# Adding a residual with accumulating scatters, and a new order on GpSimd, in a two-layer graph kernel

## The chip, the cores and the metric

The kernel runs on one core of one Trainium2 chip. The metric is the device time of one execution in microseconds (us). The core has five instruction queues of its own: TensorE (PE in the profile), VectorE (DVE), ScalarE (ACT), GpSimd (POOL) and SyncE (SP). Each works through its queue in order. DMA transfers are issued from GpSimd (all indexed ones) and from SyncE (all plain ones).

## The reference, cut to what matters

There are 16 graphs (batches) of 1024 nodes with 64 channels. Layer 0 adds a weighted mean over neighbours. Layer 1 takes, for each node and channel, three quantiles over the values of its neighbours, after some edges are removed ("dilation"), and sends the result through a small MLP. Both layers add to x.

```python
h = relu(layernorm(x))
deg = clip(sum(A, axis=2, keepdims=True), 1.0)
x = x + matmul(A / deg, h)                       # layer 0: the residual x1
h = relu(layernorm(x))
adj_d = dilate(adj, mask)                        # drops edges; the own node stays
agg = sum(w * nanquantile(h over neighbours, tau)
          for tau, w in zip([0.25, 0.5, 0.75], [0.25, 0.5, 0.25]))
y = relu((h + agg) @ W1 + b1) @ W2 + b2
x = x + y * mask                                 # the output
```

## The kernel before

**Layer 0** (`loads`, `beginnings`, `transposes`, `products`, `signs`, `listing`, `endings`, `channels`, lines 540 to 777) goes batch by batch. Rows of the adjacency matrix are loaded in eight tiles `at`; TensorE transposes them into `pt`, ScalarE copies them to `att`, TensorE multiplies by the normed x (`ps_small<-att,h`). VectorE scales, adds x and so has the residual x1. ScalarE makes signs `sg` of the rows, from which VectorE takes the largest eight keys of each of four segments (MAX8, `rec`): a list of each node's neighbours. For each node one record `row` is built (line 568): normed channels and two place holders (W = 66 columns), then x1 (64 columns, `X1`), then the list with number and mask (34 columns, `R0`), 164 in all (`RW`). The first 66 columns go to the table `tab` in HBM with a plain store (lines 710 to 712). The whole record is scattered into `srt[g]`, rows ordered by length of list (`to`, lines 773 to 775): eight indirect DMAs for each batch, 128 in all, called row scatters below. Four batches make a group (GB = 4), so there are four groups g.

**Layer 1, short lists** (`group`, line 1015). When all batches of a group are scattered, the lists come back (`recs`), the node numbers `nodes_i` are computed, GpSimd gathers the adjacency rows of the longest short lists (`gat_rows`), VectorE computes the indices `idx` and which edges go, and two indirect stores into `tab` write the dropped edges (`tab<-drop,didx`). Then ten `Job`s for each group are added (line 1126), each of T tiles of 128 nodes with n - 1 neighbours. `Job.run` (line 808) loads the own rows `S` from `srt` on SyncE, gathers T(n - 1) tiles of `places` from `tab` on GpSimd, one indirect DMA each, and then `sort` (line 840) runs a sorting network on VectorE between `places` and `other` (in PSUM) and multiplies by weights into `prod`. `layers` (line 960) does the MLP: TensorE transposes and sums `prod` into `pt`, ScalarE copies to `ot`, TensorE multiplies, ScalarE applies the activation (`hid`), TensorE multiplies, and ScalarE scales by the mask into `y`. Then VectorE adds x1 from `S` to y (line 1006) and GpSimd scatters y into the output, T indirect DMAs of 128 rows of 256 bytes (line 1011): 128 of these in all. `S` is held until the add.

**Layer 1, long lists** (`long_lists`, line 1133). Nodes with up to 88, 31, 24 and 20 neighbours, of all four groups, make four further jobs. For each, SyncE loads the records `lS`, VectorE computes `lnodes_i`, GpSimd gathers the adjacency rows (`lat`, one buffer), VectorE takes the neighbours out of them (`lkey`, `lfound`, `lkeys`, `lidx`), and a job gathers `lplaces`.

**What sets the order.** The engine queues are in order, and on VectorE and GpSimd the order is written out by the kernel's own planner (`Plan`, lines 233 to 325), when the program is built. Each piece of work is a stream that yields an engine, a time at which it may begin, and a rank. `Plan.run` always takes the stream that can begin first by the planner's clocks, and among those that can begin at the same time the one of lowest rank. Constants are slack added to the time at which an input is due: SLACK (2 us), LOOSE (15) ahead of the MLP and of the add, ROWS (7) ahead of row scatters and index gathers, LATE (25) ahead of the scatters of y. AHEAD (8) decides when a sort is urgent: `later` gives it a low rank while fewer than so many gathers are outstanding. `room(name, bufs)` holds a stream until a buffer is free.

Of the kernel before, what the change touches and what calls it, by code (L numbers as in the profile page):

```python
# [9 lines left out]
F32 = mybir.dt.float32  # L10
# [8 lines left out]
P = 128  # L19
# [189 lines left out]

INF = float("inf")  # L210
BREATH = 0.8
AHEAD = 8
SLACK = 2.0
LOOSE = 15.0
ROWS = 7.0
LATE = 25.0


class Timed:
# [13 lines left out]
class Plan:  # L233
# [132 lines left out]
def list_path(ctx, tc, x, adj, nodemask, w1, b1, w2, b2, out, go):  # L366
# [9 lines left out]
    W = C + 2  # L376
    PW = W // 2
    REC = 8 * NSEG + 2
    X1 = W
    R0 = X1 + C  # L380
    RW = R0 + REC
    NTAU = N // SUB
    NF = NG + NG + len(LONG)

# [173 lines left out]
    def beginnings(pool, now):  # L558

        for b, st in enumerate(batch):  # L560
            now[0] = b
            yield "DVE", lambda: max(known(st, "xt", "mrow"), room("h0", 3), room("row", 4))
            mrow_f = new(tiny, [NT, P], F32, "mrow_f", 2)
            nc.vector.tensor_copy(mrow_f, st["mrow"])

            h0 = new(pool, [P, NT, C + 1], F32, "h0", 3, users=2)
            nc.vector.memset(h0[:, :, C:], 1.0)
            row = st["row"] = new(pool, [P, NT, RW], F32, "row", 4, users=1)
# [89 lines left out]
    def products(pool, now):  # L658


        for b, st in enumerate(batch):
            now[0] = b
            for hf in range(2):
# [25 lines left out]
                x1 = st["row"][:, hf * BPH:(hf + 1) * BPH, X1:R0]  # L689
# [13 lines left out]
    def channels(pool, now):  # L703

        for b, st in enumerate(batch):
            now[0] = b
            row = lambda: st["row"]
            yield "DVE", lambda: known(st, "row") if st["residual"] == 2 else INF
            yield from normed(row()[:, :, :C], row()[:, :, X1:R0])
            nc.sync.dma_start(  # L710
                tab[b * TS:b * TS + N, :].rearrange("(t p) w -> p t w", p=P), row()[:, :, :W]
            )
            st["normed"] = True

    def endings(pool, now):

        for b, st in enumerate(batch):
            now[0] = b
            g, gb = divmod(b, GB)
# [51 lines left out]
            to = new(pool, [P, NT], I32, "to", 2)  # L771
            nc.vector.scalar_tensor_tensor(to, low, float(1 - GB), pos, op0=OP.mult, op1=OP.add)
            for t in range(NT):
                yield "POOL", lambda: max(at(to), at(row)) + ROWS if "normed" in st else INF
                scatter(srt[g], row[:, t, :], to[:, t:t + 1], sorts[g])
            free(row)
            progress["batches"] = b + 1

# [4 lines left out]
            in_offset=bass.IndirectOffsetOnAxis(ap=idx, axis=0),  # L783
        )

    def scatter(dst, src, idx, others):
        if plan.last is others:
            nc.gpsimd.memset(turn, 0.0)
        ins = nc.gpsimd.indirect_dma_start(
            out=dst, out_offset=bass.IndirectOffsetOnAxis(ap=idx, axis=0),  # L790
            in_=src, in_offset=None,
        )

        for other in others:
            tc.declare_no_dep(ins.ins, other, reason="rows of their own")
        others.append(ins.ins)
        plan.last = others

    class Job:
# [1 line left out]


        def __init__(self, pool, n, T, keys, idx, node, mask, nodes_i, table, S, g, name="places",
                     bufs=3, rank=0):
            self.__dict__.update(locals())
            self.short = pool is gat

        def run(self):
# [9 lines left out]
            progress["ahead"] += T * (n - 1)  # L818
            if short:
                mine = self.S  # L820
                self.S = new(pool, [P, T, R0], F32, "S", 4, users=1)
                nc.sync.dma_start(self.S, mine)
            for t in range(T):
                for k in range(n - 1):
# [11 lines left out]
        def later(self, rank):  # L836

            return rank - 900 if progress["ahead"] < AHEAD else rank + 2000

        def sort(self):  # L840
            n, T, pool, short, A, S = self.n, self.T, self.pool, self.short, self.A, self.S
# [101 lines left out]
            if short:  # L943
                free(A)
                free(Bt)
                yield "ACT", lambda: at(S)
                nc.scalar.copy(prod[:, :, count, :], S[:, :, :C])

                terms = [
                    [prod[:, t, k:min(k + 2, total), :].rearrange("p k c -> p (k c)")  # L950
                     for k in (0, *range(4, total, 2), 2)]
                    for t in range(T)
                ]
                plan.add(self.layers(terms, [prod]), -1000)
            else:
                terms = [[places(copies[k], (k, 1, 1, 1, 1))[:, 0, 0, :] for k in range(count)]
                         + [S[:, 0, :C]]]
                plan.add(self.layers(terms, [A, Bt]), -1000)

        def layers(self, terms, sources):  # L960

            T, R = self.T, terms[0][0].shape[1]
            yield "PE", lambda: max(at(*sources) + LOOSE, room("y", 6), room("pt", 2))
            y = new(mlp, [P, T, CO], F32, "y", 6, users=1)
            for t0 in range(0, T, 4):
                ts = range(t0, min(t0 + 4, T))
                M = len(ts) * P
# [34 lines left out]
                        y[:, t, :], pv[:, i, :], AF.Copy, scale=self.mask[:, t:t + 1]  # L1002
                    )
                free(py)
            yield "DVE", lambda: at(y) + LOOSE
            nc.vector.tensor_tensor(y, y, self.S[:, :, X1:R0], OP.add)
            if self.short:
                free(self.S)
            for t in range(T):
                yield "POOL", lambda: at(y) + LATE  # L1010
                scatter(out_rows, y[:, t, :], self.nodes_i[:, t:t + 1], scatters)
            free(y)
            progress["jobs"][self.g] += 1

    def group(g):
# [17 lines left out]
        )  # L1033
        nodes_i = new(grp, [P, NTAU], I32, "nodes_i", 2)
        nc.vector.tensor_copy(nodes_i, nodes)
        yield "POOL", lambda: at(nodes_i) + ROWS
        full = new(grp, [P, N], F32, "gat_rows", 1)
        gather(full, adj_rows, nodes_i[:, 0:1])
        yield "DVE", always
# [65 lines left out]
        for e in range(2):  # L1105
# [1 line left out]
                nb, cum, skip[:, e, :], None, op0=OP.is_lt, op1=OP.add,  # L1107
                accum_out=drop[:, 0, e:e + 1],
            )
        yield "POOL", lambda: at(drop) + ROWS  # L1110
        for e in range(2):
            nc.gpsimd.indirect_dma_start(
                out=pairs[:R * TS * PW, :],
# [9 lines left out]
        for i, ts in enumerate(classes):  # L1123
            n, T = CAPS[ts[0]] + 1, len(ts)
            sl = slice(ts[0], ts[-1] + 1)
            job = Job(
                gat, n, T, keys[:, sl, :n - 1], idx[:, sl, :], node[:, sl], mask[:, sl],
                nodes_i[:, sl], table, tiles[:, sl, :R0], g,
            )
            plan.add(job.run(), 100 * g + i)  # L1130
        progress["groups"] = g + 1

    def long_lists(pool):
# [4 lines left out]
        for l, K in enumerate(LONG):  # L1138
# [12 lines left out]
            nc.vector.tensor_tensor(nodes, node, noff[:, 1:2], OP.add)  # L1151
            nodes_i = new(pool, [P, 1], I32, "lnodes_i", 4)
            nc.vector.tensor_copy(nodes_i, nodes)
            yield "POOL", lambda: max(at(nodes_i) + ROWS, room("lat", 1))
            full = new(pool, [P, N], F32, "lat", 1)
            gather(full, adj_rows, nodes_i)
            yield "DVE", lambda: at(full)
# [367 lines left out]
```

## Time and profile before

Three runs took 1947.86, 1949.79 and 1966.94 us; the median is 1949.79 us. The profiled execution spans 1953.2 us.

| | TensorE | VectorE | ScalarE | GpSimd |
|---|---|---|---|---|
| busy, us | 818.3 | 1252.1 | 607.3 | 965.2 |
| share of the span | 42% | 64% | 31% | 49% |

The costliest groups on GpSimd are indirect DMAs, each as one instruction: gathers of `places` (496 of 994 ns), of `lplaces` (163 of 1057 ns), row scatters (128 of 980 ns), scatters of y (124 of 1045 ns, and four for the long lists). Busy time by slices of the span, in tenths, each slice being 48.8 us:

```profile
PE   6778651345688236611577001000001458142155
DVE  7766877636676557954642396747935779785290
ACT  7888744225465435513333000000000011010011
POOL 0123255534434654347525625478775546747723
```

A digit is the busy share of the engine in that slice. The first 22 slices hold layer 0, with the short lists of the earlier groups beside it. After that ScalarE and TensorE have little to do. In a group's row, the time after "idle before" is what the engine stood idle just ahead of those instructions, and the names after the arrow say what ended it; "issue" is a wait for nothing that the profile shows.

### The profile page before, as it was taken

What the parts mean: (1) busy time and instruction counts of PE and PEld (TensorE: products, weight loads), DVE (VectorE), ACT (ScalarE), POOL (GpSimd) and SP (SyncE); (2) the same over time, 40 slices, a digit from 0 to 9 for tenths busy, and PEclk for the clock granted to TensorE, in tenths of its full rate; (3) what the DMA queues carried; (4) which work ended last, traced back from release to release, by engine and by line L of the source; (5) the groups of instructions that cost most, each with busy time, mean ns of one, the idle gap of its engine ahead of it and who ended that gap; (6) DMA issues with size and microseconds to landing.
All of it is one profiled execution on the core that took longest, in us unless ns stands there. A gap on an engine that the chain in (4) does not pass through costs nothing.

```text
span 1953.2 us, 15147 instructions
## 1 busy us (share of the span) xinstructions
PE 818.3 (42%) x3336; PEld 518.3 (27%) x3336; DVE 1252.1 (64%) x4090; ACT 607.3 (31%) x1874; POOL 965.2 (49%) x1140
## 2 busy tenths in 40 slices
PE   6778651345688236611577001000001458142155
PEld 3334421223355013410245000000001237132134
DVE  7766877636676557954642396747935779785290
ACT  7888744225465435513333000000000011010011
POOL 0123255534434654347525625478775546747723
PEclk8978875667788678755777555555555557555556
DMA  4545633213344323422201201111111101111100
GB/s 159 160 123 167 182 103 83 64 47 75 93 123 126 91 77 117 105 74 60 56 23 37 56 19 32 30 40 22 24 27 36 25 17 25 25 43 32 24 7 14
DMA packets 119013, 129.09 MB, mean 66 GB/s; under 512 B 68306, under 2 KB 86866, under 8 KB 118914
## 3 DMA queue, kind: packets, MB, share of 16 engines
q1 hardware_dynamic: 86178, 86.58, 15.6%
q0 software_dynamic: 32736, 41.47, 9.4%
q14 instruction: 71, 0.58, 0.1%
q8 instruction: 28, 0.46, 0.1%
HBM read 108.70 MB, written 19.28 MB: 66 GB/s over the span
## 4 chain that ended last, share of the span: by engine, by line
DVE 34%; PE 16%; issue 15%; another core or an unknown queue 14%; ACT 9%; POOL 8%; DMA 2%; SPq 0%; DVEq 0%; POOLq 0%; ACTq 0%
PE ps_small L227 9%; PE pt L227 7%; DVE other L227 5%; DVE places L227 5%; DVE rec L227 4%; POOL lplaces L227 3%; POOL places L227 2%; DVE lplaces L227 2%; DVE long_other L227 2%; ACT ln_sq L227 2%; ACT sg L227 2%; DVE sg L227 2%; POOL out_dram L227 2%; ACT att L227 2%
## 5 line engine op out<-in xcount | busy, mean ns | idle before, releaser
L227 POOL DMA_INDIRECT places<-tab,idx x496 | 493.1, 994 | 263.6 <-issue 141.7
L227 PE MATMUL pt<-ident,prod 128*128 128x128 f32 (+1 forms) x736 | 155.7, 371 | 553.1 <-DVE prod L227 350.2
L227 PE MATMUL ps_small<-att,h 128*65 128x512 f32 x512 | 269.8, 677 | 63.3 <-ACT h L227 42.8
L227 PEld LDWEIGHTS pt<-ident,prod 128*128 128x128 f32 (+1 forms) x736 | 127.2, 254 | 586.0 <-issue 210.5
L227 PE MATMUL pt<-ident,at 128*128 128x128 f32 x1024 | 184.9, 329 | 170.8 <-ACT att L227 83.5
L227 POOL DMA_INDIRECT srt<-row,to x128 | 125.4, 980 | 261.0 <-ACT row L227 158.6
L227 POOL DMA_INDIRECT out_dram<-y,nodes_i x124 | 129.6, 1045 | 210.9 <-issue 72.2
L227 POOL DMA_INDIRECT lplaces<-tab,lidx x163 | 172.3, 1057 | 73.0 <-issue 47.8
L227 PEld LDWEIGHTS pt<-ident,at 128*128 128x128 f32 x1024 | 139.6, 167 | 225.0 <-ACT att L227 106.8
L227 DVE MAX8 rec<-sg 128x8 f16<-128x256 f16 x512 | 180.2, 414 | 13.2 <-remote 5.8
L227 ACT COPY att<-pt 128x512 f32<-128x512 f32 x256 | 142.3, 583 | 130.9 <-remote 79.8
L227 ACT COPY ot<-pt 128x128 f32<-128x128 f32 (+3 forms) x56 | 22.4, 399 | 426.6 <-issue 175.3
L227 ACT ACTIVATE sg<-at 128x1024 f16<-128x1024 f32 x128 | 134.9, 1055 | 40.8 <-DVE rec L227 19.0
L227 DVE TENSOR_TENSOR sg<-sg,keyed 128x1024 f16<-128x1024 f16 x128 | 87.3, 682 | 81.0 <-ACT sg L227 80.8
L227 PEld LDWEIGHTS ps_small<-att,h 128*65 128x65 f32 x512 | 78.7, 159 | 208.8 <-issue 137.8
L227 PE MATMUL ps_small<-ot,w_sb 128*128 128x128 f32 (+3 forms) x112 | 56.9, 602 | 121.7 <-ACT ot L227 89.1
L227 DVE TENSOR_TENSOR other<-places,other 128x64 f32<-128x64 f32 (+6 forms) x204 | 69.8, 342 | 39.3 <-DVE places L227 11.6
L227 PE MATMUL ps_small<-w_sb,hid 128*128 128x64 f32 x256 | 68.6, 360 | 58.4 <-issue 43.0
L227 ACT ACTIVATE y<-ps_small,recs 128x64 f32<-128x64 f32 x124 | 31.5, 312 | 187.2 <-PE ps_small L227 66.3
L227 ACT ACTIVATE wu<-wu 128x39 f32<-128x39 f32 (+9 forms) x40 | 9.4, 235 | 249.7 <-issue 130.5
L227 DVE TENSOR_TENSOR places<-places,other 128x64 f32<-128x64 f32 (+2 forms) x208 | 62.4, 309 | 25.4 <-DVE other L227 10.2
L227 PEld LDWEIGHTS ps_small<-w_sb,hid 128*128 128x128 f32 x256 | 51.1, 246 | 87.7 <-issue 53.3
(208 smaller groups left out, 1652.2 us busy)
## 6 DMA issues: line engine op xcount, KB each, us to landing
at<-in_adj_dram SPq DMA_DIRECT2D x128, 512.0 KB
places<-tab,idx POOLq DMA_INDIRECT x496
tab<-row SPq DMA_DIRECT2D x16, 264.0 KB
xt<-in_x_dram SPq DMA_DIRECT2D x16, 256.0 KB
S<-srt SPq DMA_DIRECT2D x8, 390.0 KB
lplaces<-tab,lidx POOLq DMA_INDIRECT x163
recs<-srt SPq DMA_DIRECT2D x4, 544.0 KB
S<-srt SPq DMA_DIRECT2D x8, 260.0 KB
```

Source lines behind the costliest of these rows:

```text
L227: ins = getattr(self._engine, op)(*args, **kwargs)
```

## The change

The residual x1 no longer travels with the ordered rows. When a batch's x1 is finished it is written to the output with a plain store on SyncE, 256 KB for each batch; the scatter of y becomes one that adds to what stands there (`compute_op=OP.add`), and VectorE's add goes. It is meant to take that add and its waits off VectorE. Since the scatter now depends on what was written before, it names only the part of the output up to its own group, so that it doesn't depend on batches still to come. The record is 100 columns wide for the ordered rows instead of 164, `S` 66 instead of 130, and `S` is free as soon as it has been copied into `prod`.

Beside this, `places` has four buffers instead of three and `y` four instead of six. The slack constants become one, LOOSE = 7 (from 15, 7 and 25), and the index gathers have none. AHEAD is 16. Row scatters get a rank ahead of everything that can begin at the same time (`first`), and the MLP of a short job is urgent only while fewer than 16 gathers are outstanding (`urgent`), and otherwise last; before, it always had rank -1000.

```diff
-AHEAD = 8
+AHEAD = 16
 SLACK = 2.0
-LOOSE = 15.0
-ROWS = 7.0
-LATE = 25.0
+LOOSE = 7.0
...
-    X1 = W
-    R0 = X1 + C
-    RW = R0 + REC
+    R0 = W
+    X1 = RW = R0 + REC
...
-            yield from normed(row()[:, :, :C], row()[:, :, X1:R0])
+            yield from normed(row()[:, :, :C], row()[:, :, X1:])
+
+            nc.sync.dma_start(out[b].rearrange("(t p) c -> p t c", p=P), row()[:, :, X1:])
...
+        first = lambda rank: rank - 3000
...
-                yield "POOL", lambda: max(at(to), at(row)) + ROWS if "normed" in st else INF
-                scatter(srt[g], row[:, t, :], to[:, t:t + 1], sorts[g])
+                yield "POOL", lambda: max(at(to), at(row)) + LOOSE if "normed" in st else INF, first
+                scatter(srt[g], row[:, t, :RW], to[:, t:t + 1], sorts[g])
...
-    def scatter(dst, src, idx, others):
+    def scatter(dst, src, idx, others, op=OP.bypass):
...
-            in_=src, in_offset=None,
+            in_=src, in_offset=None, compute_op=op,
...
-                     bufs=3, rank=0):
+                     bufs=4, rank=0):
...
-                self.S = new(pool, [P, T, R0], F32, "S", 4, users=1)
+                self.S = new(pool, [P, T, W], F32, "S", 4, users=1)
...
+        def urgent(self):
+            return -1000 if progress["ahead"] < AHEAD else 5000
...
                 nc.scalar.copy(prod[:, :, count, :], S[:, :, :C])
+                free(S)
...
-                plan.add(self.layers(terms, [prod]), -1000)
+                plan.add(self.layers(terms, [prod]), self.urgent)
...
-            yield "PE", lambda: max(at(*sources) + LOOSE, room("y", 6), room("pt", 2))
-            y = new(mlp, [P, T, CO], F32, "y", 6, users=1)
+            yield "PE", lambda: max(at(*sources) + LOOSE, room("y", 4), room("pt", 2))
+            y = new(mlp, [P, T, CO], F32, "y", 4, users=1)
...
-            yield "DVE", lambda: at(y) + LOOSE
-            nc.vector.tensor_tensor(y, y, self.S[:, :, X1:R0], OP.add)
-            if self.short:
-                free(self.S)
             for t in range(T):
-                yield "POOL", lambda: at(y) + LATE
-                scatter(out_rows, y[:, t, :], self.nodes_i[:, t:t + 1], scatters)
+                yield "POOL", lambda: at(y) + LOOSE
+                rows = out_rows[:min(self.g + 1, NG) * GB * N, :]
+                scatter(rows, y[:, t, :], self.nodes_i[:, t:t + 1], scatters, OP.add)
...
-        yield "POOL", lambda: at(nodes_i) + ROWS
+        yield "POOL", lambda: at(nodes_i)
...
-        yield "POOL", lambda: at(drop) + ROWS
+        yield "POOL", lambda: at(drop)
...
-            yield "POOL", lambda: max(at(nodes_i) + ROWS, room("lat", 1))
+            yield "POOL", lambda: max(at(nodes_i), room("lat", 1))
```

More of the change, by code (lines that the diff above doesn't have):

```diff
@@ L567, in beginnings @@
             nc.vector.memset(h0[:, :, C:], 1.0)
-            row = st["row"] = new(pool, [P, NT, RW], F32, "row", 4, users=1)
+            row = st["row"] = new(pool, [P, NT, X1 + C], F32, "row", 4, users=1)
             nc.vector.memset(row[:, :, C:W], -1.0)
@@ L688, in products @@
                 yield "DVE", lambda: at(pb) + SLACK
-                x1 = st["row"][:, hf * BPH:(hf + 1) * BPH, X1:R0]
+                x1 = st["row"][:, hf * BPH:(hf + 1) * BPH, X1:]
                 deg = new(tiny, [P, BPH], F32, "deg", 2)
@@ L1127, in group @@
                 gat, n, T, keys[:, sl, :n - 1], idx[:, sl, :], node[:, sl], mask[:, sl],
-                nodes_i[:, sl], table, tiles[:, sl, :R0], g,
+                nodes_i[:, sl], table, tiles[:, sl, :W], g,
             )
```

## The prediction

> **What bounds the kernel now.** I read the page's busy times and chain first, then busy time by stage, then the waits, then GpSimd's timeline where the stages meet. In the page (parts 1 and 4) the reader is to see that no engine is full and the chain is spread over all of them.
>
> ```profile
> PE 818.3 (42%) x3336; PEld 518.3 (27%) x3336; DVE 1252.1 (64%) x4090; ACT 607.3 (31%) x1874; POOL 965.2 (49%) x1140
> ...
> DVE 34%; PE 16%; issue 15%; another core or an unknown queue 14%; ACT 9%; POOL 8%; DMA 2%; SPq 0%; DVEq 0%; POOLq 0%; ACTq 0%
> ```
>
> The stages differ, so I cut the span at four events: the last row scatter (1077 us), the first sort of the 88-place list (1328), the last gather (1871), the end.
>
> ```profile
> core 0: us, PE busy (x) PEld busy (x) DVE busy (x) ACT busy (x) POOL busy (x), PEclk, DMA share, GB/s
> 0.00:1077.00 1077.00, 593.61 (x2380) 342.37 (x2380) 679.62 (x2271) 546.83 (x1681) 451.03 (x589) 0.73 0.35 97
> 1077.00:1328.00 251.00, 14.21 (x50) 11.55 (x50) 154.78 (x572) 4.93 (x18) 134.55 (x152) 0.50 0.15 35
> 1328.00:1871.00 543.00, 164.22 (x688) 128.21 (x688) 384.55 (x1149) 40.77 (x130) 354.35 (x357) 0.56 0.14 27
> 1871.00:1954.00 83.00, 46.23 (x219) 36.14 (x218) 33.15 (x99) 14.81 (x45) 25.30 (x44) 0.64 0.04 11
> ```
>
> A (layer 0 beside the short lists of three groups): four engines at 42 to 63%, held by waits for each other. B and C: VectorE and GpSimd alone, taking turns. D: a drain. The waits say how they take turns:
>
> ```profile
> POOL places L227 <- DVE prod L227: 112.2, 10, 16.7
> ...
> POOL out_dram L227 <- DVE y L227: 62.2, 5, 26.1
> ...
> DVE y L227 <- ACT y L227: 58.4, 10, 18.3
> ```
>
> GpSimd waits for a free buffer of places (112 us) and for finished y (62 us), and VectorE, in order, for y from ScalarE (58 us). Then the boundaries, in the timelines of GpSimd and VectorE:
>
> ```profile
> 1137.99 0.94 POOL L227 DMA_INDIRECT gat_rows<-in_adj_dram,nodes_i  x1 [25.31 <-DVE nodes_i L227]
> ...
> 1167.99 0.99 POOL L227 DMA_INDIRECT tab<-drop,didx  x1 [15.05 <-DVE lkeys L227]
> ...
> 1228.28 0.94 POOL L227 DMA_INDIRECT lat<-in_adj_dram,lnodes_i  x1 [16.74 <-DVE lnodes_i L227]
> ...
> 1271.96 0.94 POOL L227 DMA_INDIRECT lat<-in_adj_dram,lnodes_i  x1 [17.43 <-DVE other L227]
> ...
> 1328.41 0.34 DVE L227 TENSOR_TENSOR lrem<-lplaces,lS 128x176 f32<-128x176 f32 x1 [20.19 <-DMA lplaces<-tab,lidx]
> ...
> 1871.10 1.02 POOL L227 DMA_INDIRECT places<-tab,idx  x1 [0.30 <-issue]
> ...
> 1916.63 0.96 POOL L227 DMA_INDIRECT out_dram<-y,nodes_i  x1 [26.07 <-DVE y L227]
> ```
>
> In B GpSimd stands four times (74 us together) for indices from VectorE, and then VectorE for the last gathers of the long list. In D it stands for y.
>
> **What the Trainium skill says.** "DMA: Bandwidth & Descriptors", SWDGE vs HWDGE vs iDMA: accumulation in a DMA can only be issued by GpSimd, and a DMA operation is one read and one write descriptor. It gives no price for the added read of the destination; no run so far shows one. The same page, Rules for kernel authors: an accumulating DMA must wait for any earlier access of the same bytes; so each scatter depends on the plain write of its batches. The same page, Anatomy of one DMA: about 2.0 us fixed, mostly the receipt of the write; the trace agrees (2.18 us from the last row scatter to its landing). The same page, Specifications: under 512 B a transfer is not at line rate; row scatters go from 656 to 400 B, but the DMA share is 0.04 to 0.35, so I cost it at nothing.
>
> **The change, part by part.**
>
> The add leaves VectorE. 44 instructions of y<-y,S and y<-y,lS at a median 0.354 us and less: about 14 us of busy time. More is in the waiting: the 58.4 us above is VectorE at the head of its queue, with lists and sorts behind it. Of it 18.3 us (at 1785 to 1803) lay where VectorE starved for gathers anyway, 21 us (7.3 and 13.7) is at the very end.
>
> Residual writes: 16 plain writes of 256 KB on SyncE's queue; the rows shorten the sorted stores, and the loads of S, by about as much. DMA share at most 0.35: nothing.
>
> Stage B. I compared the built order of GpSimd's 931 indirect DMAs. The last row scatter is number 443 before, 441 after; the last gather for the 88-place list 578 and 576: the same work lies between. But the gather of the last group's adjacency rows moves from 471 to 456, its two stores from 483-484 to 474-475, the second to fourth gathers of lat from 492, 514, 535 to 483, 500, 516. On VectorE (each instruction at its row's mean) the lists now stand 25, 26 and 25 us apart, before 33, 31, 21, and the last group's nodes come 27 us of work after layer 0 instead of 41, with the first job of that group behind them. Walked from the last row scatter (t): lists load and first lnodes t+13 as now; nodes t+28 (now t+61); the two stores 26 us of work later, t+54; second lat 15 us on, t+70; the next two 25 us of list work and about 2 us of latency each, t+124; then 60 DMAs. GpSimd ran them in C at (545-94)/331 = 1.36 us each, where 94 us is its idle time over 1 us: 82 us, t+206, landed t+208. Now it is t+251. Gain 43 us; between 20 (if half is met by new stalls) and 50.
>
> Stage C. From the last gather of that list to the last gather of all: 338 DMAs instead of 331, +9.5 us. The fourth buffer of places lets GpSimd run one job further: of the 94 us idle, 56 us are waits on prod (11.8+15.2+5.3+9.3+4.5+10.0). I take off 30: VectorE must then do some 415 us in 520, 80%; from 1500 to 1800 us it reached 75 to 80%. Net -20; ends -45 and +10.
>
> Stage D. After the last gather 17 scatters remain instead of 22, and only the two smallest jobs, some 10 us of VectorE, instead of the 37 us to its last prod at 1908. The rest I take as now: 25 us from prod to y, 3 us, 9 us to the end. 2+10+25+3+9 = 49 us for 83, -34; ends -45 and -10.
>
> Stage A. Row scatters first, later layers behind gathers (urgent), slack of 7 for 15 and 25. Group 1's lists stand at 364 us of VectorE work instead of 427, so jobs spread more evenly over layer 0. Against it, TensorE meets the first prod after 7.0 batches of transposes instead of 8.0, while VectorE gets to it after the same 240 us of work; TensorE already waits 28 us there. The ends of the stage agree (700 and 709 us of VectorE work, the 8 us being adds). -10; ends -70 and +70.
>
> The accumulating scatter: 128 of them, now 0.96 us each. Lower bound: nothing, the fixed cost of issue rules. Upper: twice as much to write out, +0.96 us. I take +0.25, on the path in B to D where GpSimd is half the bound: about 63 x 0.25 = +16; ends 0 and +60.
>
> Sum: -43-20-34-10+16 = -91, so 1950-91 = 1859 us.
>
> **The rivals.** (1) The gain is hidden: VectorE's chains of small dependent steps set stage C, and GpSimd running ahead changes nothing; B gives 20, D 10, adds 5 or so: about 1925 us. For it: at 1474 to 1490 VectorE steps at 1.4 us for operations of 0.23. Against: 74 us of stalls in B have named causes that move. (2) The accumulating scatter costs double: +60 instead of +16, and A loses 35 by blocked gathers behind it: 1938 us. For it: every scatter holds GpSimd's queue. Against: gather and scatter cost the same 0.94 to 0.96 us now, whatever they move. (3) Slower: with slack of 7 GpSimd arrives at scatters whose y is late, as already at 1008 us (30.7 us of idle time), and TensorE stands at prod earlier: A +70, B to D give 35: 1985 us. For it: in A it is GpSimd's in-order waits for y that hold later gathers. Against: y no longer goes through VectorE, whose add came up to 28 us after y's first write (311.6 to 339.3).
>
> **How the numbers follow.** Forecast 0.54, hidden 0.17, double cost 0.11, slower 0.18. Faster by over 1% (below 1930): forecast and hidden, 0.71; within 1%: 0.11; slower: 0.18. The low end adds the good ends of B, C, and part of A: about 1780. The high end takes in rivals 1 and 2 and reaches into 3: 1970.
>
> **What would show it.** The last row scatter near 1067 (A), the first lrem some 208 us later (B), the last gather some 520 us after that with less wait on prod (C), the end within 50 us (D). Scatters into the output of about 1.2 us on GpSimd. No wait of VectorE on y. It is wrong if the last row scatter comes after 1110, if scatters take near 2 us, or if waits of GpSimd for y grow past what prod waits lose.

## The result and the profile after

The changed kernel took 1829.05 us (median of 4 runs, 1823.34 to 1833.25). The kernel before, run again beside it, took 1956.74 us (4 runs, 1947.86 to 1966.94). The ratio is 0.9345, with an interval from 0.9303 to 0.9387: 6.5% faster. The forecast was 1859 us with a range from 1780 to 1970, so the direction and the range held and the time came 30 us lower. The sum came out closer than its terms did.

The page of the changed kernel, engine by engine, and its group for the scatters of y:

```profile
PE 825.6 (45%) x3336; PEld 533.0 (29%) x3336; DVE 1240.1 (68%) x4046; ACT 609.3 (33%) x1874; POOL 1050.8 (58%) x1144
...
L225 POOL DMA_INDIRECT out_dram<-y,nodes_i x124 | 208.0, 1678 | 186.8 <-ACT y L225 127.4
```

VectorE has 44 instructions fewer, the adds, which took 15.2 us before; its busy time fell by 12 us. GpSimd's rose by 85.6 us: the 124 scatters now take 1678 ns each on the mean where they took 1045. The same four stages as before, cut at the last row scatter (988 us), the first `lrem` of the 88-place list (1215), the last gather (1779) and the end; the columns are the stretch, its length, and busy time and instructions of the five engines, then granted clock, DMA share and GB/s:

```profile
core 0: us, PE busy (x) PEld busy (x) DVE busy (x) ACT busy (x) POOL busy (x), PEclk, DMA share, GB/s
0.00:988.00 988.00, 588.65 (x2338) 346.35 (x2339) 674.76 (x2252) 545.00 (x1669) 486.97 (x597) 0.73 0.40 104
988.00:1215.00 227.00, 23.17 (x80) 18.13 (x79) 142.38 (x519) 7.19 (x24) 144.02 (x149) 0.51 0.18 35
1215.00:1779.00 564.00, 193.43 (x822) 151.60 (x822) 415.00 (x1251) 50.07 (x160) 389.82 (x366) 0.57 0.16 24
1779.00:1822.00 43.00, 20.37 (x98) 16.90 (x98) 7.94 (x25) 7.03 (x21) 30.02 (x34) 0.66 0.24 17
```

To the hundredth of a microsecond the ends of the stages are 988.39, 1215.40, 1779.26 and 1821.4, before 1076.93, 1328.41, 1871.10 and 1953.2:

| stage | before, us | after, us | difference | forecast |
|---|---|---|---|---|
| A | 1076.9 | 988.4 | -88.5 | -10 |
| B | 251.5 | 227.0 | -24.5 | -43 |
| C | 542.7 | 563.9 | +21.2 | -20 |
| D | 82.1 | 42.1 | -40.0 | -34 |
| price of adding, in B to D | | | in the rows above | +16 |

So A gave most, though the forecast had next to nothing there, and C got longer. The waits of GpSimd in the changed kernel (total us, times, longest):

```profile
POOL out_dram L225 <- ACT y L225: 127.4, 17, 21.1
...
POOL places L225 <- DVE prod L225: 6.1, 1, 6.1
```

and of VectorE, before and after:

```profile
DVE rem L227 <- DMA places<-tab,idx: 13.9, 1, 13.9
...
DVE rem L225 <- DMA places<-tab,idx: 90.0, 10, 25.0
```

GpSimd's wait for a free `places` buffer fell from 112.2 to 6.1 us. GpSimd now waits for y directly at ScalarE (127.4 us), and VectorE, which waited 58.4 us at the add, now waits 90.0 us for gathers (13.9 before). GpSimd's waits ahead of scatters of y, all releasers together, fell from 215.3 to 192.2 us.

The chain of waits that the profile follows back from the end breaks off at the last instruction in the changed kernel, so it can't be set beside the chain of the kernel before. GpSimd's timeline in stage B, and at the last gather:

```profile
1017.25 1.00 POOL L225 DMA_INDIRECT gat_rows<-in_adj_dram,nodes_i  x1 [2.23 <-DVE nodes_i L225]
...
1043.96 0.99 POOL L225 DMA_INDIRECT tab<-drop,didx  x1 [2.23 <-DMA places<-tab,idx]
...
1060.34 0.94 POOL L225 DMA_INDIRECT lat<-in_adj_dram,lnodes_i  x1 [3.06 <-DVE rem L225]
...
1086.66 0.94 POOL L225 DMA_INDIRECT lat<-in_adj_dram,lnodes_i  x1 [4.68 <-DVE other L225]
...
1113.51 0.94 POOL L225 DMA_INDIRECT lat<-in_adj_dram,lnodes_i  x1 [6.42 <-DVE other L225]
...
1180.01 1.63 POOL L225 DMA_INDIRECT out_dram<-y,nodes_i  x1 [10.58 <-ACT prod L225]
...
1194.64 1.58 POOL L225 DMA_INDIRECT out_dram<-y,nodes_i  x1 [12.89 <-ACT y L225]
...
1779.26 0.94 POOL L225 DMA_INDIRECT places<-tab,idx  x1 [0.30 <-issue]
1780.51 1.62 POOL L225 DMA_INDIRECT out_dram<-y,nodes_i  x1 [0.30 <-issue]
```

and VectorE's at the end of B:

```profile
1215.40 0.35 DVE L225 TENSOR_TENSOR lrem<-lplaces,lS 128x176 f32<-128x176 f32 x1 [26.86 <-DMA lplaces<-tab,lidx]
```

The four stalls of 15 to 25 us in the earlier timeline are gone: the largest of the first five idle times is 6.42 us. But the scatters of y at 1180 and 1194 us stand ahead of the last gathers of the 88-place list; waits and scatters together take 10.58 + 1.63 + 12.89 + 1.58 = 27 us there, and VectorE waits 26.86 us for those gathers. At the end the scatter of y follows the last gather at once, where GpSimd stood idle 26.07 us before its scatter at 1916 us in the kernel before.

### The profile page after: what moved, and what is told of

It reads as the page before. It is cut to its first block, busy times and chain, and to the rows that moved or that the text cites. A ratio compares the mean times of both kernels' runs of the same rounds, so it can differ in the third digit from the quotient of the medians.

```text
span 1821.4 us, 15210 instructions
## 1 busy us (share of the span) xinstructions
PE 825.6 (45%) x3336; PEld 533.0 (29%) x3336; DVE 1240.1 (68%) x4046; ACT 609.3 (33%) x1874; POOL 1050.8 (58%) x1144
## 5 line engine op out<-in xcount | busy, mean ns | idle before, releaser
L225 PE MATMUL pt<-ident,prod 128*128 128x128 f32 (+1 forms) x736 | 161.8, 384 | 569.4 <-DVE prod L225 294.5
L225 POOL DMA_INDIRECT out_dram<-y,nodes_i x124 | 208.0, 1678 | 186.8 <-ACT y L225 127.4
L225 PEld LDWEIGHTS pt<-ident,prod 128*128 128x128 f32 (+1 forms) x736 | 134.2, 267 | 605.3 <-issue 389.7
L225 POOL DMA_INDIRECT srt<-row,to x128 | 129.4, 1011 | 259.0 <-ACT row L225 223.5
L225 PE MATMUL pt<-ident,at 128*128 128x128 f32 x1024 | 190.0, 334 | 179.6 <-ACT att L225 72.1
L225 PE MATMUL ps_small<-att,h 128*65 128x512 f32 x512 | 259.0, 652 | 17.7 <-ACT h L225 10.3
L225 PEld LDWEIGHTS pt<-ident,at 128*128 128x128 f32 x1024 | 143.5, 171 | 236.5 <-ACT att L225 97.7
L225 PE MATMUL ps_small<-w_sb,hid 128*128 128x64 f32 x256 | 72.5, 376 | 52.6 <-ACT hid L225 25.1
L225 PEld LDWEIGHTS ps_small<-w_sb,hid 128*128 128x128 f32 x256 | 53.6, 258 | 80.5 <-ACT hid L225 40.3
L225 DVE TENSOR_TENSOR rem<-places,recs 128x30 f32<-128x30 f32 (+9 forms) x40 | 7.3, 182 | 101.7 <-DMA places<-tab,idx 90.0
L225 POOL MEMSET turn<- 128x1 f32 x204 | 76.2, 373 | 0.1
```

Source lines behind the costliest of these rows:

```text
L225: ins = getattr(self._engine, op)(*args, **kwargs)
```

## The experiments

**The questions.** My theory was that the order on GpSimd gives the gain (lists and long gathers earlier, in B and D; the fourth buffer in C) and that adding costs little. The rivals: the price of adding is large and eats the gain; or the gain is that of taking the add off VectorE. A fourth theory came up with the first runs, that the gain depends on the chip.

**The chips.** The experiments ran on three chips. On chips P and Q the kernel before takes 1592 to 1597 us, on chip R 1981, and on the chip of the first traces ("the first chip" below) 1957. Which one that was isn't known; it may have been R. A time is therefore compared only with the kernel before on its own chip, by the ratio.

### The two kernels on chip P

No edit: both kernels as they are.

> The kernel before, for its trace on the same chip as the experiments. Theory: no unnamed waits; the stage to the last row scatter is shorter by 200 us or more than on record, because that stage needs all five engines in turn; the later stages by less. Rival 'everything is stretched alike': every stage at 0.81 of its recorded length.

> The changed kernel itself, on the chip of this set of runs. In the first set the kernel before took 1594 us where the recorded comparison had 1957; the sizes of single instructions were the same, but waits of ScalarE and VectorE that the trace cannot name (464 us in all, 347 in the changed kernel) were gone. Theory 'the fourth buffer carries most of what is left': with three buffers 0.996 of before, so with four 0.97-0.98. Rival 'the gain is mostly less exposure to those unnamed waits': 0.99-1.00 here, though 0.9345 on record. Rival 'nothing of the chip matters': 0.93-0.94.

Measured: the kernel before 1595.16 us (one run; 24 runs beside it have a median of 1596.91), the changed kernel 1588.87 (12 runs), ratio 0.9955 [0.9941, 0.997]. Here the change gains 0.45%, not 6.5%. Windows by stage, the kernel before on chip P:

```profile
0.00:855.00 855.00, 569.73 (x2380) 334.65 (x2380) 678.69 (x2271) 544.53 (x1681) 461.42 (x589) 0.80 0.43 123
855.00:1071.00 216.00, 14.21 (x50) 11.56 (x50) 154.10 (x572) 4.93 (x18) 134.02 (x152) 0.50 0.17 40
1071.00:1538.00 467.00, 165.67 (x723) 131.17 (x724) 409.40 (x1223) 44.09 (x140) 360.55 (x356) 0.57 0.15 31
1538.00:1594.00 56.00, 35.22 (x185) 27.35 (x184) 7.60 (x25) 11.59 (x35) 24.77 (x45) 0.71 0.06 16
```

and the changed kernel on chip P:

```profile
0.00:830.00 830.00, 563.98 (x2380) 336.36 (x2380) 672.69 (x2252) 547.15 (x1681) 494.16 (x599) 0.81 0.48 124
830.00:1031.00 201.00, 10.04 (x36) 8.28 (x36) 142.43 (x519) 3.26 (x12) 145.03 (x147) 0.50 0.21 40
1031.00:1546.00 515.00, 192.98 (x822) 150.80 (x822) 415.15 (x1252) 50.21 (x160) 390.63 (x367) 0.57 0.18 26
1546.00:1588.00 42.00, 18.81 (x98) 15.68 (x98) 7.30 (x24) 6.92 (x21) 29.60 (x34) 0.66 0.26 17
```

In stage A VectorE is busy 678.7 us here and was busy 679.6 us in the first trace, but the stage is 855 us long and not 1077. Over the whole kernel before, VectorE is busy 1250 us here and 1252 there, ScalarE 605 and 607, GpSimd 981 and 965. On these three engines the work is the same; what differs is idle time. TensorE is busy 785 us here and 818 there, at a clock granted to it of 0.69 and 0.65 of full speed on the mean (in stage A 0.80 and 0.73). These 33 us are part of the difference, but can't be all of 360 us. The packets of the two large DMA queues (q1 and q0 of the page) took 30.2% of 16 engines' span here and 25.0% there, which is 481 and 488 us: the packets themselves took as long. How the idle time looks can be seen at one and the same job. In the kernel before, on the chip of the first traces, the last transposes of `prod` and ScalarE's copy of them (timelines of TensorE and of ScalarE):

```profile
1519.68 4.76 PE L227 MATMUL pt<-ident,prod 128*128 128x128 f32 x24 [19.04 <-DVE prod L227]
...
1539.21 0.58 ACT L227 COPY ot<-pt 128x512 f32<-128x512 f32 x1 [32.83 <-remote]
```

and on chip P:

```profile
1224.59 5.18 PE L227 MATMUL pt<-ident,prod 128*128 128x128 f32 x24 [19.03 <-DVE prod L227]
...
1229.81 0.58 ACT L227 COPY ot<-pt 128x512 f32<-128x512 f32 x1 [18.60 <-PE pt L227]
```

On chip P ScalarE starts 0.04 us after the transposes end (1229.77). In the first trace they end at 1524.44 and ScalarE starts 14.8 us later, and the profile can't name what ended the wait ("remote"). I call these unnamed waits. The first trace has 464 us of them in 82 waits (ScalarE 317, VectorE 147; they overlap, so they don't add up to lost time), the changed kernel's 347 us in 77, and no trace of chips P and Q has one. They are not all of it: waits of over 1 us on ScalarE and VectorE that end in "issue", which is nothing that the profile shows, come to 477 us in the first trace and 150 in the changed kernel's, and on chip P to none and 8 us. What stops the engines was not found.

The stages on the two chips, from the same events:

| stage | before: first chip / P | changed: first chip / P | change on first chip | change on P | rest |
|---|---|---|---|---|---|
| A | 1076.9 / 854.5 | 988.4 / 829.8 | -88.5 | -24.7 | -63.8 |
| B | 251.5 / 216.8 | 227.0 / 201.6 | -24.5 | -15.2 | -9.3 |
| C | 542.7 / 467.1 | 563.9 / 514.2 | +21.2 | +47.1 | -25.9 |
| D | 82.1 / 54.9 | 42.1 / 41.5 | -40.0 | -13.4 | -26.6 |
| sum | 1953.2 / 1593.3 | 1821.4 / 1587.1 | -131.8 | -6.2 | -125.6 |

The last column says: of the recorded gain 6 us are there on a chip without unnamed waits, and 126 us are time that the kernel before loses on the first chip and the changed one doesn't (360 against 234 us). The unnamed waits point the same way: 292 us before and 210 after in A, 157 and 113 in C. In D there are 2 and 0. There the first chip leaves over work, with VectorE busy 33.2 us in D of the kernel before against 7.6 on chip P. That the unnamed waits cause the difference between the chips is argued from these sums; no run shows it.

### The price of adding

```diff
-                scatter(rows, y[:, t, :], self.nodes_i[:, t:t + 1], scatters, OP.add)
+                scatter(rows, y[:, t, :], self.nodes_i[:, t:t + 1], scatters)
```

> The changed kernel with plain scatters of y in place of the adding ones; x1 is not added to the rows that are scattered, all else and the order of every engine's instructions are the same. It measures the price of adding. In the changed kernel one adding scatter holds GpSimd 1.68 us against 1.05 before, 0.63 us x 128 = 81 us. Theory (GpSimd is half the bound after layer 0, where 77 of the 128 lie): scatters fall back to about 1.05 us and the time falls by 20 to 48 us, to 1780-1810 us. Rival (the price is hidden behind VectorE): 1820-1830 us, unchanged.

This kernel leaves out the adding of x1, so it is a measure of the price and no kernel to use. Measured on chip P: 1548.86 us, ratio 0.9715 [0.9687, 0.9742]. Instructions on the output in the changed kernel, with their durations in ns (least, median, largest), and first and last start:

```profile
L225 POOL DMA_INDIRECT out_dram<-y,nodes_i x124: 1562/1586/2745, 284.6 to 1578.1; - x124
```

and with plain scatters:

```profile
L225 POOL DMA_INDIRECT out_dram<-y,nodes_i x124: 956/974/4161, 280.8 to 1539.5; - x124
```

An adding scatter of 128 rows of 256 bytes takes 1.59 us of GpSimd at the median, a plain one 0.97. Over 128 of them GpSimd is busy 1059.4 us instead of 982.6, 77 us more, and the span is 38.6 us longer: 14.4 in A, 4.1 in B, 14.3 in C, 5.8 in D. Half of the price reaches the end. The Trainium skill, "Perfetto Trace Analysis", section "DMA Instruction — SWDGE (GPSIMD)", says that the recorded end of such an instruction is when its descriptors are written, not when the data has moved; by that, the 0.6 us are GpSimd's own time and not the transfer's. The traces agree in two things. The next scatter waits its turn: in a run of them at 809.61 and 811.53 us the starts are 1.92 us apart, with a small memset between. And there is more to write out for an adding scatter. The queue of GpSimd's DMAs (packets, MB, share of 16 engines) in the changed kernel and with plain scatters:

```profile
q0 software_dynamic: 45024, 37.28, 14.5%
...
q0 software_dynamic: 30688, 37.28, 10.8%
```

The bytes are the same, but the adding scatters make 14336 packets more, 112 for each of the 128. In the packets themselves each adding scatter goes out as 128 of 256 bytes, one for each row, and each plain one as 16 of 2048 bytes, eight rows in one. That the 0.6 us go into these 112 packets fits, but no run here separates it from the adding as such.

So without the price the change would gain 2.9% on chip P; the price takes 2.4 of it.

### The two halves of the change alone

The residual part alone (kernel before, with the narrow rows, the plain store of x1, no add on VectorE, adding scatters; slack, ranks and buffers as before):

```diff
-            yield "DVE", lambda: at(y) + LOOSE
-            nc.vector.tensor_tensor(y, y, self.S[:, :, X1:R0], OP.add)
...
-                scatter(out_rows, y[:, t, :], self.nodes_i[:, t:t + 1], scatters)
+                rows = out_rows[:min(self.g + 1, NG) * GB * N, :]
+                scatter(rows, y[:, t, :], self.nodes_i[:, t:t + 1], scatters, OP.add)
```

> The kernel before with the first part alone: x1 written to the output by batch, adding scatters, no add on VectorE, records of 100 columns, S free once it is copied. All slack constants, AHEAD, ranks and the three places buffers as before. Theory (both parts matter; the adds with their waits on VectorE are worth some 60 us and the adding scatters cost some 40): about 1930 us. Rival 'the residual is the gain': 1840-1870 us. Rival 'the order is the gain, the residual only costs GpSimd time': 1980-2000 us.

Measured on chip P: 1662.84 us, ratio 1.0438 [1.0411, 1.0464]. Stages 908.2, 212.7, 488.3 and 50.9 us: A is 53.6 us longer than in the kernel before, C 21.3. The planner, which doesn't know the price, puts 62 scatters of y ahead of the last row scatter instead of 45.

The order part alone (slack, ranks, four buffers of y; x1 in the rows, VectorE's add, plain scatters):

```diff
-AHEAD = 8
+AHEAD = 16
-LOOSE = 15.0
-ROWS = 7.0
-LATE = 25.0
+LOOSE = 7.0
...
-                yield "POOL", lambda: max(at(to), at(row)) + ROWS if "normed" in st else INF
+                yield "POOL", lambda: max(at(to), at(row)) + LOOSE if "normed" in st else INF, first
...
-                plan.add(self.layers(terms, [prod]), -1000)
+                plan.add(self.layers(terms, [prod]), self.urgent)
```

`places` keeps three buffers in it; with the wide rows a fourth doesn't fit.

> The changed kernel with the add back on VectorE, plain scatters, no write by batch, records of 164 columns, and three places buffers (with records this wide a fourth does not fit). Slack of 7, AHEAD 16, row scatters first and urgent as in the changed kernel. Theory: about 1880 us. Rival 'the order is the gain': 1830 us or less, since it is spared the price of the adding scatters. Rival 'the residual is the gain': 1940-1960 us.

Measured on chip P: 1598.14 us, ratio 1.0039 [1.0016, 1.0063]. VectorE's wait for y in stage C, in the kernel before on chip P (1071 to 1538 us) and in this one (1032 to 1547 us):

```profile
DVE y L227 <- ACT y L227: 3.4, 2, 3.0
...
DVE y L225 <- ACT y L225: 56.7, 10, 11.2
```

With short slack VectorE arrives at the add before y is there, ten times. Stages 818.4, 214.1, 514.4 and 48.5 us: against the kernel before on chip P, A is 36 us shorter and C 47 longer. C is as long in the changed kernel (514.2 us), which has no add on VectorE: there VectorE waits for gathers in its place (64.9 us for those of `places` and 38.6 for those of `lplaces`). So the lack of the add doesn't shorten C; what the changed kernel has over the order part alone are 13 us in B and 7 in D, less 11 in A.

Each half alone loses, 4.4 and 0.4%, and both together gain 0.45%: they depend on each other, and neither's effect can be read from the sum. Both orders were written anew by the planner, though, and telling the planner another price (below) moves the time by 3.6% through the order alone. So the 4.4% are those of one order with the residual part in it, and not the price of that part as such.

### The fourth buffer

```diff
-                     bufs=4, rank=0):
+                     bufs=3, rank=0):
```

> The changed kernel with three places buffers instead of four; the order of every engine's instructions is the same, so only the waits differ. Theory (the fourth buffer takes away GpSimd's waits on prod, 112 us in all before): waits of places on prod of 60-110 us come back and the time rises by 20-50 us, to 1850-1880 us. Rival (GpSimd's waits for a buffer were off the path): 1829 us, within 8.

Measured on chip P: 1587.18 us, ratio 0.9961 [0.995, 0.9971], with the changed kernel at 0.9955. The instructions stand in the same order on every engine, and GpSimd has no wait for `places` on `prod` in either. On chip P the buffer is worth nothing that these intervals can tell.

It looks different where there are unnamed waits. There, with three buffers, GpSimd waited for `prod` 112.2 us (kernel before, first chip) and 81.3 us (the version with TensorE's add below, chip R); with four, 6.1 us (changed, first chip), 24.8 and 7.3 us (the two runs below on chip R). On chips P and Q the five kernels with three buffers waited 0 to 16.7 us. The Trainium skill, "Perfetto Trace Analysis", section "Optimization Strategy", reads a gap that repeats on the engine that should be full as a possible lack of room for the next tile. GpSimd is busy only 49 to 67% of the span, but its gaps for `prod` fit this, on some chips only. The changed kernel with three buffers was not run on such a chip, so what the buffer is worth there in time is not shown.

### Three ways to pay less for the add

The planner is told a price of 1.9 us for an adding scatter, in place of 1.27:

```diff
+            if kwargs.get("compute_op") == OP.add:
+                time = 1.9
```

> The changed kernel with the planner told what an adding scatter costs on GpSimd (1.9 us between issues, measured: 1.58 and 0.3) in place of 1.27. All else the same; the order is written anew. Theory (the planner's order is off where scatters come in rows, by 0.6 us each): 5 to 20 us faster than the changed kernel. Rival: within 5 us, or slower by chance of the order.

Measured on chip P: 1645.71 us, ratio 1.0313 [1.0288, 1.0337]. A miss. Stages 794.2, 264.7, 533.3 and 48.9 us: A is 35.7 us shorter than in the changed kernel, B 63.1 longer, C 19.1, D 7. A truer price on one instruction moved 40 indexed DMAs, ten scatters of y among them, out of A, where GpSimd has time to spare (busy 494 of 830 us), into B (177 instead of 137). Why C is longer with the same number was not found.

GpSimd adds x1 with an instruction of its own and scatters plainly (x1 in the rows, loaded into a tile of its own; three buffers of y, and a price for the add in the planner):

```diff
+            yield "POOL", lambda: at(y, x1) + LOOSE
+            nc.gpsimd.tensor_tensor(y, y, x1 if self.short else self.S[:, :, X1:], OP.add)
```

> The changed kernel with the add as an instruction of GpSimd ahead of plain scatters: x1 stays in the ordered rows (164 columns) and comes back in a small tile of its own, so that the fourth buffer still fits; y has three buffers instead of four; no write by batch, no adding scatters. Theory (the price of the adding scatter, 81 us of GpSimd time, is partly on the path; 44 adds of about 0.3 to 1 us on GpSimd cost some 25 us instead): near the kernel with plain scatters (0.9715 of before), 0.97-0.98. Rival (adds on GpSimd wait for y and hold up the gathers as VectorE's did its own queue): 0.99-1.01.

Measured on chip P: 1592.2 us, ratio 0.9985 [0.9967, 1.0003]. Its 44 adds take 28 us of GpSimd (26.4 and 1.5), against 77 for adding in the scatters; yet it isn't faster. B is 241 us instead of 201.6, A 804 instead of 829.8: the order moved as well, so this compares two orders as much as two adds. Inconclusive.

TensorE adds, by two multiplications with the identity into PSUM:

```diff
+                nc.tensor.matmul(zv, ident, yt.rearrange("p t c -> p (t c)"), start=True, stop=False)
+                nc.tensor.matmul(zv, ident, rest.rearrange("p t c -> p (t c)"), start=False, stop=True)
+                yield "ACT", lambda: at(pz) + SLACK
+                nc.scalar.copy(yt.rearrange("p t c -> p (t c)"), zv)
```

> A version that pays for the residual on an engine with room: x1 travels with the ordered rows again and is loaded by a plain transfer into a tile of its own; TensorE adds y and x1 by two multiplications with the identity into PSUM, ScalarE copies the sum back, and GpSimd scatters it without adding. Slack 7 becomes 10, places has three buffers and y six, so that the last row scatter stays at number 441. If GpSimd's price for adding (some 80 us of its time) and VectorE's wait at the add are what the two other places of the add cost, then both go: 1550 to 1575 us, near the run with plain scatters and no x1 (1549), at a ratio to the kernel before of 0.97 to 0.985. If the longer chain from prod to y (about 2 us more per job, through two engines that work in order) comes back as stalls of TensorE in layer 0: 1585 to 1610.

This and the next two ran on chip R, so the times named there don't apply and the ratios do. Measured: 1905.93 us, ratio 0.9585 [0.9503, 0.9666], where the changed kernel had 0.9345 on the first chip. GpSimd's waits:

```profile
POOL places L225 <- DVE prod L225: 81.3, 4, 27.5
```

It has three buffers of `places`, and GpSimd waits for them. As a ratio it lies below the range of 0.97 to 0.985 that I gave for the price and VectorE's wait both gone, but that range was made for chip P, and a ratio can't be carried from one kind of chip to the other. It doesn't beat the changed kernel, and whether it would with four buffers was not tried.

### Slack, and the rank of the MLP

The old slack constants in the changed kernel:

```diff
-LOOSE = 7.0
+LOOSE = 15.0
+ROWS = 7.0
+LATE = 25.0
```

> The changed kernel with the three old slack constants back (15 us ahead of the MLP, 7 ahead of row scatters and index gathers, 25 ahead of the scatters of y); all else of the change stays. In the built order the last group's adjacency gather and the second to fourth long-list gathers come 12, 14, 19 and 24 instructions later on GpSimd, the last row scatter comes 4 earlier. Theory one, the short slack pays where I said, in stage B: B grows from the 201 us of the changed kernel to some 217, as in the kernel before on this chip, and A, C and D stay: 1600 to 1610 us. Theory two, the order on GpSimd is worth little on this chip, as the run of the order part alone said: 1580 to 1595.

Measured on chip R: 1894.67 us, ratio 0.958 [0.9505, 0.9656]. Its windows by stage:

```profile
0.00:1035.00 1035.00, 600.73 (x2328) 342.02 (x2328) 673.08 (x2252) 542.19 (x1663) 480.94 (x587) 0.73 0.38 99
1035.00:1297.00 262.00, 31.20 (x102) 24.19 (x102) 155.95 (x569) 10.19 (x36) 163.46 (x175) 0.50 0.19 34
1297.00:1819.00 522.00, 175.38 (x749) 135.79 (x749) 407.35 (x1209) 45.43 (x143) 374.70 (x351) 0.57 0.17 24
1819.00:1869.00 50.00, 33.67 (x159) 27.45 (x158) 4.70 (x18) 10.25 (x32) 31.30 (x36) 0.65 0.23 15
```

Against the changed kernel on the first chip B is 34 us longer (262 for 227; the kernel before had 251), C 42 shorter, A 47 longer. GpSimd's wait on ScalarE's y is 45.1 us instead of 127.4. This has the direction of theory one in B, but doesn't show it. With this order 156 indexed DMAs lie in B instead of 138, and 320 in C instead of 335, so that part of both differences is work that moved; and B has 97 us of unnamed waits here, where the changed kernel's trace has 24. What the run does show is that 4.2% are gained here without the short slack. The kernel before is 1.2% slower on chip R than on the first chip, some 12 us of a stage A, which doesn't explain the 47.

The MLP of short jobs always first, as before:

```diff
-                plan.add(self.layers(terms, [prod]), self.urgent)
+                plan.add(self.layers(terms, [prod]), -1000)
```

> The changed kernel with the MLP of a short job always at rank -1000, as before the change. In the built order 63 scatters of y instead of 51 then come ahead of the last row scatter, which is number 478 of the indirect DMAs instead of 443. Theory one, work only moves from C to A while GpSimd sets both: A longer by 35 DMAs of some 1.6 us, 55 us, C shorter by less because VectorE sets it there: 1605 to 1640 us. Theory two, A has GpSimd time to spare, so pulling 12 adding scatters into it takes their price off the later stages: A longer by under 20 us, C and D shorter by 25 or more: 1570 to 1585.

Measured on chip R: 1869.43 us, ratio 0.9427 [0.9377, 0.9477]. Stages 1070, 236, 503 and 59 us against 988, 227, 564 and 42: A 82 longer, B 9, C 61 shorter, D 17 longer. Work moves from C into A (475 indexed DMAs in A instead of 440, 296 in C instead of 335) and by the sizes doesn't come free there, as in theory one. But A has 271 us of unnamed waits against 210, so that what the moved work costs isn't settled. The new rank is worth under 1%, at the edge of what these intervals tell.

### The order part once more

> The order part alone once more (slack constants, ranks of row scatters and of the MLP, four buffers of y; x1 in the rows, VectorE's add and the plain scatters as before), on a chip where the unnamed waits of the first traces are present, as they were in the runs with the old slack and with the old rank of the MLP (0.958 and 0.943 times the kernel before). The whole change gave 0.9345 on such a chip and 0.9955 on one without those waits, where the order part alone gave 1.004. Theory one, order: work made ready earlier is what is worth more where engines stop at random, so the order part alone gives most of the gain here: 0.94 to 0.965. Theory two, the residual part: VectorE, which must wait at the add for a y that comes late through TensorE and ScalarE, is what such stops hit, so without the residual part little is left: 0.985 to 1.01. If the chip is again one without those waits: 1.002 to 1.006, and the question stays open.

Measured, on chip Q: 1596.59 us, ratio 1.0025 [1.001, 1.004] (22 runs). Chip Q has no unnamed waits. The ratio is the one that I expected for such a chip. It repeats chip P's 1.0039, and leaves open which half carries the gain where such waits are.

## Why the prediction was right, and where it was not

The direction and the range were right, on the first chip. Set against chip P the sum of -91 us would have missed by far, with -6 measured; a forecast from chip P's own trace would have had other waits to start from (0.6 us on `prod` in C, where I had 56) and was not made. The forecast leaned, without saying so, on a profile in which "another core or an unknown queue" had 14% of the chain of waits.

- **Stage A, -10: wrong.** Measured -88.5, beyond my good end of -70, and -24.7 on chip P. The step was "the ends of the stage agree (700 and 709 us of VectorE work, the 8 us being adds)". Equal work says nothing of a stage that is 1077 us long with 680 us of VectorE in it. Of the 112 us that GpSimd waited for `prod`, 56 lay in A (at 294, 334, 732 and 778 us), and I counted the fourth buffer in C alone. On chip P, without unnamed waits, A takes 855 us: on the first chip the kernel before loses 222 us more in A, the changed one 159. That the buffer is what saves the difference fits the waits, but was not isolated. On chip P it isn't the buffer: there the order part alone, with three buffers, takes 36 us off A, where I had 10 for all of it.
- **Stage B, -43: right in its mechanism, a term left out.** The second, third and fourth long-list gathers came 72, 98 and 125 us after the last row scatter, where I had t+70 and t+124; the stores came at t+56, where I had t+54. But the list was ready at t+227 and not t+208. In the 60 gathers at 1.36 us I had left out the two scatters of y among them, which wait and take 27 us.
- **Stage C, -20: wrong sign.** Measured +21.2. The step was "56 us are waits on prod ... I take off 30". Those 56 us went, as foreseen. In their place GpSimd waits for y: in C 16.6 us on VectorE's y became 62.5 on ScalarE's and 10.5 on `prod`. GpSimd's waits in C, before and after:

```profile
POOL places L227 <- DVE prod L227: 56.0, 6, 15.2
...
POOL out_dram L227 <- DVE y L227: 16.6, 2, 13.1
...
POOL out_dram L225 <- ACT y L225: 62.5, 6, 14.0
```

And the 47 scatters there take 83.2 us where 41 took 48.1. This is the mechanism of the third rival, in C and not in A. On chip P, where there were no 56 us to win, C grew by 47.1, of which 14.3 are the price; the order part alone, at plain prices, has the same growth.
- **Stage D, -34: right.** Measured -40.0; 42 us where I had 49, with the 17 scatters that I counted. On chip P D gives 13.4: the 37 us to VectorE's last `prod` that I took off are work that the first chip had left over.
- **The adding scatter, +16: mechanism right, size off.** I took +0.25 us each; it is +0.63 (0.96 to 1.58 us at the median), between my ends of 0 and 0.96 and nearer to the upper. My upper end took twice as much to write out; it is eight times as many packets, at a smaller price. On chip P it costs 24 us in B to D and 39 in all, since A pays too, which I had left out. The range of 0 to 60 held it.
- **The add on VectorE, residual writes.** VectorE has no wait on y left, as I said, and the plain stores of x1 show up in no wait of any size. The three signs of failure that I gave did not come: the last row scatter came at 988 us, a scatter takes 1.58 and not 2 us, and the waits for y grew by 65 us while those for `prod` lost 106.
- **The rivals.** The first (hidden gain, 1925) and the second (double cost, 1938) had part of their mechanisms right, the second a price of two thirds of what it assumed. On chip P the result is nearest to the second by its number, but not by its mechanism: A gained there, where the second rival had it lose.

The sum came right because A's error (-78) and those of C (+41, with the price in it), B (+18) and D (-6) partly cancel: -25 together, and with the 16 us of price that I had counted beside the stages -41, from -91 to -132. (These are differences of the profiled executions; the medians differ by 128.) That is luck in the terms.

## What to carry to other kernels

Moving an operation to another engine is first a question of its price there: adds that took 15 us of VectorE became 77 us more on GpSimd, and half of that reached the end on chip P. Slack, rank and buffers of a written-out order work together with the waits that instructions make on in-order engines; halves of such a change, run alone, need not add up to the whole. And where a profile has a large share of waits that it can't name, the gain of deeper buffering or earlier issue may belong to that chip: run both kernels on a second one before putting a number to the change.

## What the runs showed that I had not expected

An indirect scatter that adds takes 1.56 us of GpSimd at the least, a plain one 0.95, at 128 rows of 256 bytes; it goes out as 128 packets, the plain one as 16. The Trainium skill, "DMA: Bandwidth & Descriptors", section "SWDGE vs HWDGE vs iDMA", says that only GpSimd can issue a DMA that adds, and gives no price; this is one.

The same kernel takes 1592 to 1597 us on two chips and 1957 to 1981 us in two sets of runs elsewhere, with the same busy time on VectorE, ScalarE and GpSimd to within 2% in the two traces of it (TensorE 785 and 818 us). The slower traces have 347 to 519 us of waits without a named releaser, up to 34.5 us long, mostly ScalarE after TensorE; the quicker ones have none. The cause stays open.
